# Attention weights of two head groups in six blocks: exponentials from query-by-key scores, turned in 32 by 32 squares and gathered through DRAM

## Chip, core and metric

The kernel runs on one core of one Trainium2 chip. The time is the device time of one execution in microseconds; the median of the runs shown stands for the kernel. The core has a matmul engine (PE, with PEld its weight loads), VectorE (DVE), ScalarE (ACT), GpSimd (POOL) and SyncE (SP), which issues nearly all DMAs of this kernel; 16 DMA engines move the data.

## What is computed

One transformer block with adaptive layer norm, in float32, on 8 sequences of 1024 tokens and 512 features; 16 heads of 32 features each, causal attention, a hidden layer of 2048 with gelu.

```python
mod = silu(cond) @ Wada + bada                     # 8 x 3072, split in six
sh_a, sc_a, gt_a, sh_m, sc_m, gt_m = split(mod, 6)
xm = layernorm(x, g1, be1) * (1 + sc_a) + sh_a
q, k, v = split_heads(xm @ Wqkv)                   # 16 heads of 32
scores = where(causal, q @ k.T / sqrt(32), -inf)
x = x + gt_a * (merge_heads(softmax(scores) @ v) @ Wproj + bproj)
xm = layernorm(x, g2, be2) * (1 + sc_m) + sh_m
x = x + gt_m * (gelu(xm @ W1 + b1) @ W2 + b2)
```

## The kernel before

**Tiling.** The 8 sequences are cut into 16 blocks of 512 tokens; block n is half h = n % 2 of sequence n // 2. A block of half 0 attends to its own 512 keys alone, in a causal triangle; a block of half 1 also to the 512 keys before. The 16 heads form four groups g of four heads (4 × 32 = 128 partitions). Queries, keys (`qTs`, `kTs`) lie features on partitions, values (`vs`) tokens on partitions. The large matrices (projections, hidden layer) run as Strassen products on halves, in the helper of L217, with weights streamed through a ring of 8 tiles of 256 KB (`wp`, fetched on SP at L358 to L362).

**An order written at build time.** All loops run in Python while the program is built. The instructions of each engine are laid down in one order that is fixed then, by a planner: `now` holds a modelled time of each engine and of the DMA queue, `written` and `left` when a datum is ready or free, `note`, `note_pe`, `note_act`, `note_dma` (L90 to L135) advance them with durations written in by hand. A DMA is modelled as beginning 1.0 us after its issue, landing 1.2 us after its transfer. Work that may wait is a generator (`start`, `sides`); it yields what it needs next. `work` (L1423) advances the thread with the shortest modelled wait. `step_aside` (L1457) and `until` lay linear work (matrices) in front of a piece of attention that isn't ready, and `pace` spreads a block's attention over the linear work planned for it (`planned_time`). On the chip each engine then runs its own instructions strictly in this order, and a semaphore that isn't there yet stops the engine.

**Attention before.** For each group the scores are computed twice. First by query (`scores_at_once`, L1595): 128 queries on partitions, keys along the row, in a PSUM buffer `st` of 4 heads × 512 columns; VectorE adds the triangle mask (L1607) and takes the row maxima (L1610). The maxima are split into three bf16 parts (`split_maxima`, on POOL or DVE) and turned by small matmuls (`maxima_rows`, L1648), so that they lie along the queries. Then by key (`weights_T`): keys on partitions, queries along the row; the matmuls of L1674 put the negative maxima into `st`, those of L1686 add the scores, ScalarE takes one exponential over 128 x 2048 (L1698) into an SBUF buffer `pT` (three slots, `free_p`), POOL cuts the triangle (L1703). This orientation is what the product with the values needs (`weigh`, L1726, into PSUM `po`). POOL adds the weights of all key tiles (`add_weights`, L1816); in `finish` a matmul with ones sums them over the keys (L1747), ScalarE copies sum and values to SBUF (L1756, L1759), VectorE inverts in four pieces (L1765), POOL multiplies (L1790) into `qTs`, from where the output projection reads.

**Units.** In a triangle the widths are 512, 384, 256 and 128 columns per head. They are packed into `st` as units: 512; 384 + 128; and one that two neighbouring groups share, 256 + 256. So a pair of groups in a block of half 0 has five units by query and five by key.

**DRAM detours that are there already.** `turn` (L700 to L714) turns normalized rows in 32 by 32 squares on VectorE, writes them to DRAM in one DMA of 1 MB (`held`) and reads them back in four of 256 KB.

Of the kernel before, what the change touches and what calls it, by code (L numbers as in the profile page):

```python
# [9 lines left out]
F32 = mybir.dt.float32  # L10
# [12 lines left out]
def kernel(  # L23
# [413 lines left out]

    cond_act = tmp.tile([P, TB], F32, tag="top", name="cond_act", bufs=1)[:B, :]
    nc.scalar.activation(cond_act, cond_sb, AF.Silu)
# [113 lines left out]
    def add_job(job, reads, first=False):  # L553

        at = sum(1 for other in jobs if other[2]) if first else len(jobs)
        jobs.insert(at, (job, reads, first))

    def run_jobs(everything=False):
# [37 lines left out]
    def hurry():  # L596

        while jobs and due(jobs[0][1]) <= now["PE"] + 500:
# [881 lines left out]
    TRIANGLE = [[0], [1, 3], [2]]  # L1480
    groups = [(n, g) for n in range(NB) for g in range(NC)]

# [175 lines left out]

    free_p = list(range(3))
    first_end, unadded = (0, NC - 1), []  # L1660
    outs, totals = {}, {}

    def weights_T(n, g, parts):
# [18 lines left out]
        for k, c0, w, gg in parts:  # L1682
# [53 lines left out]
    def finish(n, g):  # L1736
# [7 lines left out]
        for i, (c0, w, term, held) in enumerate(terms):  # L1744
# [6 lines left out]
            note_pe(2 * COLUMN * w, "columns", [("acc", n, g), ("p", held)], [("l", bank)])  # L1751
        free_p.extend([slot, *(held for *_, held in more)])
        top = tmp.tile([P, TB], F32, tag="top", name=f"top_{n}_{g}", bufs=1)
        rec = tmp.tile([P, TB], F32, tag="rec", name=f"rec_{n}_{g}", bufs=1)
        kr = "rec"
# [20 lines left out]
        if (n, g) == first_end:  # L1776
# [5 lines left out]
            return  # L1782

        def quotient():
            invert(3)
# [33 lines left out]
    def attend():  # L1819
        previous = None  # L1820
        for n in range(NB):
            h = blocks[n][1]
            slots = []
            mine = sum(exp_need(parts) for g in range(NC) for parts in weight_units(n, g))
            for g in range(NC):
                nxt = groups.index((n, g)) + 1
                n_slots = len(weight_units(n, g))

                over = n_slots - 1 if g % 2 == 0 else n_slots
                for k in range(n_slots):  # L1830
                    upto = len(units)
                    if nxt < len(groups):
# [4 lines left out]
                        if k == n_slots - 1 and nxt + 1 < len(groups):  # L1837
# [3 lines left out]
            stream["rate"] = planned_time(n) / mine * (0.7 if n == 0 else 1.0)  # L1841
            written["free for k", n + 2 if n % 2 else n + 1] = 0.0
# [31 lines left out]
    def close(n, g, parts, pT, slot, last):  # L1874

        until(lambda: n - blocks[n][1] + parts[-1][0] // NTT in valued)
        own, other = [[part for part in parts if (part[3] == g) == of] for of in (True, False)]
        weigh(n, g, own, pT, slot, last)
        if other:
            shared[n, g + 1] = other, pT, slot  # L1880
        elif parts[0][0] > 0 and (n, g) != first_end:
            free_p.append(slot)
        if parts[0][0] == 0:
            totals[n, g] = (pT, slot)
            if (n, g) in shared:
                more, pT, slot = shared.pop((n, g))
                weigh(n, g, more, pT, slot, False)
                add_weights(n, g, more, pT, slot)
                if (n, g) != first_end:
                    free_p.append(slot)  # L1890
        if last:
            finish(n, g)

    def next_scores():
# [15 lines left out]

    needs = sum(exp_need(parts) for n in range(NB) for g in range(NC) for parts in weight_units(n, g))
    needs += sum(score_need(*unit) for unit in units)
    for n in range(NB):
# [80 lines left out]
```

## Time and profile before

| | |
|---|---|
| runs of the kernel | 3505.2, 3508.09, 3507.78 us; median 3507.78 |
| profiled execution | 3510.74 us, its span 3509.0, granted PE clock 0.998 |
| instructions | 120365 |
| DMA | 491.10 MB, mean 140 GB/s |
| share of the 16 DMA engines, SP's queue | 47.1% |

The profile's page gives busy time by engine, then groups of instructions by source line; the chain of waits follows the work that ended last back from release to release; a view by stretches gives busy time of each engine in a window, with clock, DMA share and GB/s; a timeline lists instructions in order, start and duration in us. A float32 matmul appears as two instructions, and four heads run side by side in 32-row or 32-column parts of the array, so one piece of a unit is 8 matmul instructions (4 in bf16). The duration of a matmul contains the depth of the pipeline; what it costs in a stream is read from start to start.

### The profile page before, as it was taken

What the parts mean: (1) busy time and instruction counts of PE and PEld (TensorE: products, weight loads), DVE (VectorE), ACT (ScalarE), POOL (GpSimd) and SP (SyncE); (2) the same over time, 40 slices, a digit from 0 to 9 for tenths busy, and PEclk for the clock granted to TensorE, in tenths of its full rate; (3) what the DMA queues carried; (4) which work ended last, traced back from release to release, by engine and by line L of the source; (5) the groups of instructions that cost most, each with busy time, mean ns of one, the idle gap of its engine ahead of it and who ended that gap; (6) DMA issues with size and microseconds to landing.
All of it is one profiled execution on the core that took longest, in us unless ns stands there. A gap on an engine that the chain in (4) does not pass through costs nothing.

```text
span 3509.0 us, 120365 instructions
## 1 busy us (share of the span) xinstructions
PE 3454.3 (98%) x54429; PEld 1724.0 (49%) x54429; DVE 2198.9 (63%) x2401; ACT 1212.4 (35%) x1276; POOL 2084.2 (59%) x2258
## 2 busy tenths in 40 slices
PE   8999999999999999999999999999999999999999
PEld 4444445445554545445454454544555444554445
DVE  5766676564666656665666566765666756656563
ACT  2335333342233423335223342333423343232531
POOL 3767846666366663756727576275753658537660
PEclk9999999999999999999999999999999999999999
DMA  6843444535545445363454534545354544443334
GB/s 212 263 137 104 137 115 140 142 107 159 142 125 156 119 147 153 119 170 115 137 157 130 155 117 144 150 137 148 116 155 137 165 122 146 128 136 101 96 121 140
DMA packets 328194, 491.10 MB, mean 140 GB/s; under 512 B 27260, under 2 KB 177596, under 8 KB 324100
## 3 DMA queue, kind: packets, MB, share of 16 engines
q1 hardware_dynamic: 327568, 483.39, 47.1%
q8 instruction: 428, 7.01, 0.8%
q14 instruction: 82, 0.67, 0.1%
q10 hardware_dynamic: 116, 0.03, 0.0%
HBM read 425.57 MB, written 55.64 MB: 137 GB/s over the span
## 4 chain that ended last, share of the span: by engine, by line
PE 83%; POOL 7%; DMA 3%; DVE 3%; ACT 1%; issue 1%; SPq 1%; ACTq 0%; DVEq 0%; POOLq 0%
PE bank L217 59%; PE sc L1595 8%; PE st L1686 6%; PE po L1726 6%; POOL pT L1816 4%; PE st L1674 2%; PE bank L1747 2%; DMA hat_m<-held_m 1%; DVE mx L1610 1%; POOL hT L170 1%; ACT pT L1698 1%; DMA held_m<-xm_m 1%; PE bank L1648 0%; POOL xr L170 0%; DMA w<-in_L_cond_Wqkv_dram 0%
## 5 line engine op out<-in xcount | busy, mean ns | idle before, releaser
L1816 POOL TENSOR_TENSOR pT<-pT,pT 128x256 f32<-128x256 f32 (+3 forms) x1254 | 1219.7, 1007 | 298.5 <-PE po L1726 181.6
L1698 ACT ACTIVATE pT<-st 128x2048 f32<-128x2048 f32 x288 | 540.9, 1878 | 1065.1 <-PE st L1686 959.8
L217 PE MATMUL bank<-w,hT 128*32 128x256 f32 x14336 | 823.7, 380 | 0.4 <-issue 0.4
L1610 DVE TENSOR_REDUCE mx<-sc 128x4 f32<-128x2048 f32 (+3 forms) x384 | 665.9, 1755 | 235.6 <-PE sc L1595 229.5
L217 PEld LDWEIGHTS bank<-w,hT 128*32 128x32 f32 x14336 | 446.7, 110 | 390.3 <-issue 105.8
L217 PE MATMUL bank<-xm_m,w 128*32 128x256 f32 x8192 | 498.6, 381 | 3.6 <-ACT xm_m L774 2.2
L217 PE MATMUL bank<-t_m,w 128*32 128x256 f32 x6144 | 382.4, 380 | 0.9 <-DVE t_m L786 0.6
L217 PEld LDWEIGHTS bank<-xm_m,w 128*32 128x32 f32 x8192 | 255.6, 110 | 231.2 <-issue 62.2
L1703 POOL TENSOR_SCALAR_AFFINE_SELECT pT<-pT 128x512 f32<-128x512 f32 x256 | 167.5, 672 | 331.9 <-ACT pT L1698 329.4
L1607 DVE TENSOR_TENSOR sc<-sc,mask 128x1024 f32<-128x1024 f32 (+1 forms) x160 | 162.8, 1018 | 293.3 <-PE sc L1595 237.8
L1595 PE MATMUL sc<-kT,qT 32*128 32x512 f32 (+3 forms) x3072 | 329.5, 521 | 4.3 <-ACT pT L1698 3.3
L1726 PE MATMUL po<-pT,v 128*32 128x512 f32 (+3 forms) x3048 | 301.6, 490 | 3.9 <-POOL pT L1703 3.9
L1686 PE MATMUL st<-qT,kT 32*128 32x512 f32 (+3 forms) x3072 | 300.8, 487 | 0.0
L217 PEld LDWEIGHTS bank<-t_m,w 128*32 128x32 f32 x6144 | 189.6, 110 | 172.9 <-issue 48.5
L1765 DVE RECIPROCAL rec<-rec 128x128 f32<-128x128 f32 x256 | 227.3, 922 | 48.2 <-ACT rec L1756 48.2
L217 PE MATMUL bank<-xm_a,w 128*32 128x256 f32 x3968 | 243.4, 382 | 0.4 <-DMA w<-in_L_cond_Wqkv_dram 0.4
L217 PE MATMUL bank<-w,qT 128*32 128x512 f32 x2048 | 237.0, 595 | 1.1 <-DMA w<-in_L_cond_Wproj_dram 0.7
L1595 PEld LDWEIGHTS sc<-kT,qT 32*128 32x128 f32 x3072 | 129.6, 183 | 188.2 <-issue 88.4
L208 DVE TENSOR_TENSOR hT<-bank,u_u 128x512 f32<-128x512 f32 x187 | 126.6, 686 | 105.8 <-PE bank L217 103.1
L217 PE MATMUL bank<-t_a,w 128*32 128x256 f32 x2944 | 183.2, 380 | 0.0
L217 PEld LDWEIGHTS bank<-xm_a,w 128*32 128x32 f32 x3968 | 123.5, 110 | 110.3 <-issue 29.3
L1115 ACT ACTIVATE hT<-hT,cols 128x512 f32<-128x512 f32 x256 | 164.7, 712 | 35.9 <-DVE hT L208 28.5
(243 smaller groups left out, 3404.0 us busy)
## 6 DMA issues: line engine op xcount, KB each, us to landing
w<-in_L_cond_W_dram SPq DMA_DIRECT2D x384, 256.0 KB
w<-kept_up_S SPq DMA_DIRECT2D x256, 256.0 KB
w<-kept_down_S SPq DMA_DIRECT2D x256, 256.0 KB
w<-kept_qkv_S SPq DMA_DIRECT2D x180, 256.0 KB
w<-in_L_cond_Wqkv_dram SPq DMA_DIRECT2D x147, 256.0 KB
hat_a<-in_x_dram SPq DMA_DIRECT2D x64, 256.0 KB
xr<-in_x_dram SPq DMA_DIRECT2D x32, 512.0 KB
w<-in_L_cond_Wproj_dram SPq DMA_DIRECT2D x64, 256.0 KB
```

What stands on the lines that cost most here:

```text
L208: nc.vector.tensor_tensor(out, src, other, op)
L217: nc.tensor.matmul(ps[r, :], columns, rhs, start=start, stop=stop, skip_group_check=True)
L1115: nc.scalar.activation(hT[:, i, :], hT[:, i, :], AF.Gelu, bias=cols[:, O_B1 + f : O_B1 + f + 1])
L1595: nc.tensor.matmul(sc[:, j, c0 : c0 + w], qTs[n][r, gg, ts(qt, P)], keys_of(n, kh)[r, gg, :w], start=True, stop=True, skip_group_check=True,)
L1607: nc.vector.tensor_tensor(place, place, shape_of.to_broadcast(place.shape), ALU.add)
L1610: nc.vector.tensor_reduce(maxima[n, gg][:, kh, qt, :], sc[:, :, c0 : c0 + w], axis=AX.X, op=ALU.max)
L1686: nc.tensor.matmul(st[:, j, c0 : c0 + w], kT[r, gg, ts(k % NTT, P)], qT[r, gg, TB - w :], start=False, stop=True, skip_group_check=True,)
L1698: nc.scalar.activation(pT[:, :, :used], st[:, :, :used], AF.Exp, scale=scale)
L1703: nc.gpsimd.affine_select(diagonal, diagonal, pattern=[[0, HPG], [1, P]], compare_op=ALU.is_ge, fill=0.0, base=0, channel_multiplier=-1,)
L1726: nc.tensor.matmul(po[r, TB - w :], v[:, k % NTT, g * P + j * hd : g * P + (j + 1) * hd], pT[:, j, c0 : c0 + w], start=(k == 0), stop=last ...
L1765: nc.vector.reciprocal(some, some)
L1816: nc.gpsimd.tensor_tensor(into, into, pT[:, j, c0 : c0 + w], ALU.add)
```

## The change

For groups 0 and 1 of the blocks n = 4, 6, 8, 10, 12, 14 (`row_groups`), the weights are taken from the scores by query, and the scores by key are not computed. Of each row unit (`rows_unit`): scores by query, mask and maxima as before; then ScalarE takes one exponential per head and part, with the negative maximum as bias and the row sum as a second output, written so that 32 by 32 squares are in place; VectorE turns all squares of 128 x 2048 (`turned`); SP writes them in four DMAs of 256 KB to a DRAM image and reads the image back in one DMA of 1 MB into a slot of `pp` (`spread_unit`), whose layout has keys on partitions; the values are multiplied in pieces of 128 columns. The row sums are inverted and spread along the queries through DRAM, five small DMAs per group (`inverses`), and one product per group with the inverse ends it (`finish_rows`). So for these groups the subtracted maxima, second scores, triangle cuts, additions on POOL, sums by ones and long reciprocals are gone.

The row units run at the start of their block (`attend_rows`) over a share of 0.45 of its planned time; groups 2 and 3 follow as before, and their first values wait in the plan for the row groups' end (`close`). The three slots are shared. For all blocks the rule by which VectorE's waiting jobs are laid down (`run_jobs`) is looser: up to 2 us ahead of PE's modelled time. `top` and `rec` become halves of one buffer.

```diff
     def run_jobs(everything=False):
+        run_row_jobs(everything)
         while jobs and (
-            everything or (now["DVE"] <= now["PE"] and due(jobs[0][1]) <= now["PE"])
+            everything or (now["DVE"] <= now["PE"] + 2000 and due(jobs[0][1]) <= max(now["PE"], now["DVE"]))
         ):
...
-    groups = [(n, g) for n in range(NB) for g in range(NC)]
+    def row_groups(n):
+        return (0, 1) if n > 3 and blocks[n][1] == 0 else ()
...
+    groups = [(n, g) for n in range(NB) for g in range(NC) if g not in row_groups(n)]
...
-        slot = free_p.pop(0)
+        until(lambda: free_p)
+        slot = take_slot()
...
         until(lambda: n - blocks[n][1] + parts[-1][0] // NTT in valued)
+        if by_rows(n):
+            until(lambda: (n, row_groups(n)[-1]) in gathered)
...
+    SHARE = 0.45
...
+    def rows_unit(n, g, parts):
+        until(lambda: n in projected)
+        until(lambda: free_p and len(raws) < 2)
...
+        for i, (qt, kh, c0, w, gg) in enumerate(parts):
+            nc.vector.tensor_reduce(mx[:, i, :], sc[:, :, c0 : c0 + w], axis=AX.X, op=ALU.max)
+            note("DVE", 170 + 4.14 * w, ["st"], [("mxr", slot)])
+        nc.vector.tensor_scalar(minus[:, :n_parts], mx[:, :n_parts], -scale, None, ALU.mult)
...
+            for j in range(HPG):
+                nc.scalar.activation(
+                    tile_of[:, j], sc[:, j, c0 : c0 + w].rearrange("p (k b x) -> p k b x", b=NTT, x=hd),
+                    AF.Exp, bias=minus[:, i, j : j + 1], scale=scale, accum_out=totals_of[n, gg][:, j, qt : qt + 1],
+                )
+                note_act(480 + 0.82 * w, "exp", ["st", ("mxr", slot)], [("p", slot)])
...
+        def turned():
+            nc.vector.transpose(raw, raw)
+            note("DVE", 2320, [("p", slot)], [("p", slot)])
+            written["p", slot] += 1500
+            start(spread_unit(n, raw, slot, parts, order_of[n, g, parts[0][0]]))
+        row_jobs.append((turned, [("p", slot)]))
+
+    def spread_unit(n, raw, slot, parts, i):
+        yield [("p", slot)], []
+        image = kept.tile([P, NTT, TB], F32, tag=f"image_{i % 5}", name=f"image_{n}_{i}")
+        for a in range(NTT):
+            into = image[:, a, :].rearrange("(b x) r -> x b r", x=hd)
+            nc.sync.dma_start(into, raw[ts(a, hd)].rearrange("x (b r) -> x b r", b=NTT))
+            note_dma(700, [("p", slot)], [("image", n, i)])
+        left["p", slot] = now["DMA"] + LAND
+        written["image", n, i] += 1500
...
+        page = pp.tile([P, NTT, TB], F32, tag=f"p{taken_slot}", name=f"turned_{n}_{i}")
+        nc.sync.dma_start(page, image)
+        note_dma(2700, [("image", n, i)], [key])
+        written[key] += 2000
+        if i:
+            yield [("valued rows", n, i - 1)], []
+        for qt, kh, c0, w, gg in parts:
...
+            for k in range(w // P):
...
+                for j in range(HPG):
+                    r = slice(j * hd, (j + 1) * hd)
+                    at = c0 + k * P + j * hd
+                    nc.tensor.matmul(
+                        out[0][r, ts(qt, P)],
+                        vs[n][:, k, gg * P + j * hd : gg * P + (j + 1) * hd],
+                        page[:, :, at : at + hd],
+                        start=out[1] == 1,
+                        stop=out[1] == 10,
+                        skip_group_check=True,
+                    )
+                note_pe(2 * COLUMN * P, "columns", [key], ["po"])
+            if out[1] == 10:
+                finish_rows(n, gg, out[0])
...
+    def inverses(n, g):
...
+        nc.vector.reciprocal(some, some)
...
+        nc.vector.transpose(both[:, 1, :].rearrange("p (y i) -> p y i", i=hd), wide)
...
+            nc.sync.dma_start(both[ts(j, hd), 0, :], row.to_broadcast([hd, TB]))
...
+    def finish_rows(n, g, out):
+        into = qTs[n][:, g, :]
+        if wait_of(([("inverses", n, g)], [])) > 0 or max(now["DVE"], due(["po"])) > max(now["ACT"], due(["po"])) + 2500:
+            nc.scalar.copy(into, out)
+            note_act(585, None, ["po"], [("values", n, g)])
+            start(scaled(n, g, into))
+        else:
+            nc.vector.tensor_tensor(into, out, inverse_rows.pop((n, g)), ALU.mult)
```

More of the change, by code (lines that the diff above doesn't have):

```diff
@@ new lines, in row_need, with attend_rows @@
+    def row_need(n, g, parts):
+        return score_need(n, g, parts) + 400 + 1900 * sum(part[3] for part in parts) / TB
+    def attend_rows(n, previous):
+        todo = row_units(n)
+        lo = unit_at[0]
+        more = MORE
+        ends = [lo + i * 0 // (len(todo) - 1) for i in range(len(todo))]
+        mine = sum(row_need(n, *unit) for unit in todo)
+        mine += sum(score_need(*unit) for unit in units[lo : ends[-1]])
+        stream["rate"] = SHARE * planned_time(n) / mine
+        written["free for k", n + 1] = 0.0
+        for g in row_groups(n):
+            written["spread", n, g] = NEVER
+            written["sums", n, g] = NEVER
+            written["inverses", n, g] = NEVER
+            in_sums[n, g] = 0
+        for (g, parts), upto in zip(todo, ends):
+            rows_unit(n, g, parts)
+            run_excursions(1)
+            pace(row_need(n, g, parts))
+            if previous is not None:
+                close(*previous)
+                previous = None
+                for i in (n, n + 1):
+                    written["free for v", i] = 0.0
+            while unit_at[0] < upto:
+                ns = score_need(*units[unit_at[0]])
+                next_scores()
+                run_excursions(1)
+                pace(ns)
+            maxima_rows()
@@ new lines, in inverses @@
+    def inverses(n, g):
+        before = [("spread", n, g - 1)] if g else []
+        yield [("sums", n, g), "top used", *before], ["top", "rec"]
+        both = tmp.tile([P, 2, TB], F32, tag="top", name=f"inverse_{n}_{g}", bufs=1)
+        some = totals_of.pop((n, g))
+        nc.vector.reciprocal(some, some)
+        note("DVE", 170, [("sums", n, g)], [("sums", n, g)])
+        wide = some.rearrange("p j t -> p (j t)").unsqueeze(2).to_broadcast([P, HPG * NTT, hd])
+        nc.vector.transpose(both[:, 1, :].rearrange("p (y i) -> p y i", i=hd), wide)
+        note("DVE", 700, [("sums", n, g)], ["rec"])
+        yield ["rec"], []
+        rows = kept.tile([HPG, NTT, NTT, hd], F32, tag=f"inverse_{g % 2}", name=f"inverse_rows_{n}_{g}")
+        nc.sync.dma_start(
+            rows.rearrange("j t a i -> a (j t) i"),
+            both[0:P:hd, 1, :].rearrange("a (y i) -> a y i", i=hd),
+        )
+        note_dma(150, ["rec"], [("rows back", n, g)])
+        yield [("rows back", n, g)], []
+        for j in range(HPG):
+            row = rows[j : j + 1].rearrange("j t a i -> j (t a i)")
+            nc.sync.dma_start(both[ts(j, hd), 0, :], row.to_broadcast([hd, TB]))
+            note_dma(200, [], ["top"])
+        inverse_rows[n, g] = both[:, 0, :]
+        written["inverses", n, g] = written["top"] + LATE / 2
```

139 lines of the change are left out of this document (126 added, 13 removed).

## The prediction

> **What bounds the kernel now.** I read the page first, then the busy time by stretches, then the TensorE timeline of some units.
>
> ```profile
> span 3509.0 us, 120365 instructions
> ...
> PE 3454.3 (98%) x54429; PEld 1724.0 (49%) x54429; DVE 2198.9 (63%) x2401; ACT 1212.4 (35%) x1276; POOL 2084.2 (59%) x2258
> ...
> DMA packets 328194, 491.10 MB, mean 140 GB/s; under 512 B 27260, under 2 KB 177596, under 8 KB 324100
> ...
> PE 83%; POOL 7%; DMA 3%; DVE 3%; ACT 1%; issue 1%; SPq 1%; ACTq 0%; DVEq 0%; POOLq 0%
> ```
>
> The matmul engine is busy 98% of the span and makes 83% of the chain that ended last; no other engine reaches 65%. The stretches say whether that holds where the change acts. Below are the stretch from 500 to 3350 us, then the sum row of six stretches in which groups 0 and 1 of blocks 4, 6, 8, 10, 12 and 14 run today (from the end of the block before to the end of group 1: 770 to 870, 1200 to 1295, and so on, 561 us together).
>
> ```profile
> 500.00:3350.00 2850.00, 2832.54 (x44551) 1411.91 (x44544) 1780.19 (x1915) 1007.55 (x1056) 1714.17 (x1846) 1.00 0.47 137
> ...
> 1200.00:1295.00 95.00, 94.53 (x1546) 48.79 (x1536) 56.91 (x56) 26.43 (x25) 75.44 (x73) 1.00 0.49 151
> ...
> sum 561.00, PE 556.56 PEld 278.91 DVE 338.17 ACT 160.24 POOL 438.95; mean PE 92.76 PEld 46.48 DVE 56.36 ACT 26.71 POOL 73.16
> ```
>
> PE idles 17.5 of 2850 us in the middle and 4.4 of 561 us in the six stretches, at clock 1.00. So a microsecond of matmul taken out there is a microsecond of time, as long as PE finds its next work ready. Busy ends are modelled, so I price by start-to-start, not by busy.
>
> **What is removed from PE.** Per pair of groups five key-by-query score units with the subtracted maxima (L1674, L1686), two sums by ones (L1747), two turns of the maxima (L1648). From the PE timeline, a unit of each shape and the next start:
>
> ```profile
> 976.07 0.40 PE L1674 MATMUL st<-mrow,minus_ones 32*128 32x384 bf16 x8
> ...
> 977.32 0.64 PE L217 MATMUL bank<-t_m,w 128*32 128x256 f32 x8
> ...
> 980.36 0.41 PE L1648 MATMUL bank<-ident_b,mcols 128*32 128x128 bf16 x16
> 980.59 1.47 PE L1726 MATMUL po<-pT,v 128*32 128x512 f32 x16
> ```
>
> ```profile
> 1051.81 0.40 PE L1674 MATMUL st<-mrow,minus_ones 32*128 32x256 bf16 x8
> ...
> 1053.00 1.92 PE L217 MATMUL bank<-w,qT 128*32 128x512 f32 x16
> ...
> 1059.51 0.40 PE L1674 MATMUL st<-mrow,minus_ones 32*128 32x512 bf16 x4
> ...
> 1060.69 1.50 PE L217 MATMUL bank<-w,qT 128*32 128x512 f32 x12
> ```
>
> The 384+128 unit takes 977.32 − 976.07 = 1.25 us, the shared 256+256 unit 1053.00 − 1051.81 = 1.19, the 512 unit 1060.69 − 1059.51 = 1.18; a pair has two, one and two: 2 × 1.25 + 1.19 + 2 × 1.18 = 6.05. A turn of maxima takes 980.59 − 980.36 = 0.23. The ones-sum has its price in the chain of waits:
>
> ```profile
> 1054.93 0.86 PE po L1726 x16
> ...
> 1066.91 0.86 PE bank L1747 x8
> ```
>
> 0.86 each. Per pair: 6.05 + 2 × 0.23 + 2 × 0.86 = 8.23 us; six pairs: **49.4 us**.
>
> **What is added to PE.** The scores by query (L1595) are computed as before, once, so they cost nothing new. The values (L1726) keep their columns: ten pieces of 128 per head and group in place of 512+384+256+128, both 1280. A pair's five units, 512 columns a head each, cost 5 × 0.86 = 4.3 today. Twenty pieces of 128 at a quarter of 0.86 (0.215) are 4.3 again; that a 128 behind a 384 already costs no more is the x16 line (0.86 for 384+128). The upper bound is the busy time of the single 128 form:
>
> ```profile
> L1726 PE MATMUL po<-pT,v 128*32 128x128 f32 x504 | 25.3, 273 | 0.2 <-POOL pT L1703 0.2
> ```
>
> 25.3 us over 63 sets of eight is 0.40 each, so 20 × 0.40 = 8.0: at worst +3.7 a pair, +22 in all. I take 0: the turns of L1648 put four sets of 128 columns, sixteen weight loads, into 0.23 us, so loads at this rate are not the limit there (they are bf16, which is why the upper end stays in the range). Reading the page in runs of 32 elements shows in no row; it belongs to the same bounds.
>
> The Trainium skill (TensorE: Matmul & The Clock Gate, Back-to-back issue gap) gives for streams of weight load and matmul about 81 ns at 128 columns against 56 ns alone. By that ratio, as an estimate, the pieces would cost 1.45 times as much, 6.2 us a pair, and the sum would be 12 us worse; the trace's 128 columns behind 384 do not show it, and a row of 128s after another is not in this trace.
>
> **What is added elsewhere, and hidden.**
>
> ```profile
> L1816 POOL TENSOR_TENSOR pT<-pT,pT 128x256 f32<-128x256 f32 (+3 forms) x1254 | 1219.7, 1007 | 298.5 <-PE po L1726 181.6 <-ACT pT L1698 114.5
> L1698 ACT ACTIVATE pT<-st 128x2048 f32<-128x2048 f32 x288 | 540.9, 1878 | 1065.1 <-PE st L1686 959.8 <-POOL pT L1816 54.1 <-POOL mcols L1631 23.7
> ...
> L1765 DVE RECIPROCAL rec<-rec 128x128 f32<-128x128 f32 x256 | 227.3, 922 | 48.2 <-ACT rec L1756 48.2
> ...
> L1115 ACT ACTIVATE hT<-hT,cols 128x512 f32<-128x512 f32 x256 | 164.7, 712 | 35.9 <-DVE hT L208 28.5 <-POOL hT L170 6.7
> ...
> L700 DVE STREAM_TRANSPOSE xm_a<-hat_a 128x512 f32<-128x512 f32 x56 | 35.1, 674 | 0.0
> ```
>
> ScalarE: five exponentials of 1.88 become 32 small ones a pair with a bias per row. L1115 has such a bias: 0.712 at 512 wide; 2048 wide at 1.878 bounds the slope at 0.78 to 0.92 ns an element, so 384, 256 and 128 come to about 0.60, 0.49, 0.38, and the 32 to 8 × 0.71 + 8 × (0.60 + 0.38) + 8 × 0.49 = 17.4 us. The read-out of the sums has no row: 0 to 0.2 us each, 0 to 6. Less 9.4 for the old ones: +8 to +14 a pair, in a stretch where ACT is busy 160 of 561 us. Hidden.
>
> VectorE: five turns of 2048 at 4 × 0.674 = 2.7 (13.5), against eight reciprocals of 0.92 (7.4); with the small inverse and two products about +9 a pair, on 338 of 561 busy. Hidden by matmuls in other banks; without that cover it would be the 54 us of six pairs. POOL loses 24 additions at about 1.0, eight triangle cuts and two products, some 30 us a pair: worth nothing directly, since PE hardly waits for it.
>
> The score buffer (one, tag "st") is now held through the exponentials, 2.9 us for the 512 unit and 3.9 for the others; in exchange the second unit's 1.2 on PE and 1.9 on ACT no longer take it: about level.
>
> DMA: each of 30 units writes 1 MB of squares in four transfers and reads 1 MB back, plus five small ones per group: 210 more issues on SP, at 0.42 as below 88 us of a queue that otherwise waits for free ring pieces. The nearest rows are today's turns of x through DRAM (one write of 1 MB, four reads of 256 KB); SP's issues, the chain, and what PE lost:
>
> ```profile
> 1255.43 0.42 SPq L709 DMA_DIRECT2D held_a<-xm_a  x1
> ```
>
> ```profile
> 1255.43 5.38 DMA held_a<-xm_a
> ...
> 1263.06 6.04 DMA hat_a<-held_a
> 1269.25 2.23 ACT xm_a L774 x3
> ```
>
> ```profile
> 1274.26 3.66 PE L217 MATMUL bank<-w,xm_a 128*32 128x256 f32 x64 [0.47 <-ACT p_v L197]
> ```
>
> That trip took 13.8 us (1255.43 to 1269.25) against 12.0 in the planner's figures (1.0 + 2.6 + 1.2 and 1.0 + 4 × 1.25 + 1.2), and PE lost 0.47. The new trip runs the other way: the first leg is four writes from 32 partitions each, like today's reads, the second one transfer of 1 MB, like today's write. Planned are 1.0 + 4 × 0.7 + 1.2 + 1.5 and 1.0 + 2.7 + 1.2 + 2.0 = 13.4 us with their margins, so at today's 13.8 it would overrun by 0.4, not by 1.8. Two waits are new. On SP the read of a page waits for its image to land; behind it stand weight loads, for which PE waits, but the ring holds eight pieces of 32 instructions each, 1.8 us a piece by the last row (64 in 3.66), 14 us in all. On PE the first value matmul of a unit waits for its page, and everything in order on PE stands behind it. I take 0.5 us of lost PE a unit, next to the 0.47, since the smaller overrun meets a busier queue: 15 us. Bounds: 0, and 0.8 (all 17.5 us of middle idle over the 22 or so trips there), 24 us.
>
> The planner's looser rule for VectorE's jobs touches all 16 blocks; I take 0, between a gain of the few microseconds idle and a loss of the same.
>
> **Sum.** −49.4 + 0 + 15 = −34.4 us, against the profiled execution's 3510.7 (its span plus 1.7): 3476.3. That execution is 3.0 above the median of the runs, so 3507.8 − 34.4 = **3473**.
>
> **Rivals.** *Late pages (slower).* PE's order is fixed beforehand, so a page later than planned is lost PE time, 30 times. 491 MB take 47% of 3509 us today, 3.4 us a MB; 10.5 MB a pair in about 93 us add 0.38 to a share of 0.48: 0.86. If that stretches a trip by a fifth (13.8 to 16.4 us) and PE pays the whole overrun, it loses 3 us a unit, 90 in all: 3507.8 − 49.4 + 90 = 3548. It decides from 49.4 / 30 = 1.65 us a unit. For it: the plan leaves no room at share 0.49. Against, too, that an overrun of 1.8 cost PE only 0.47 above. And the busiest 50 us for DMA behind the first 200 leave PE no idle time:
>
> ```profile
> 800.00:850.00 50.00, 49.97 (x884) 28.22 (x884) 29.88 (x31) 9.40 (x11) 34.95 (x33) 1.00 0.69 210
> ```
>
> *Attention falls behind (no change).* Values of groups 2 and 3 now wait in the plan for the last row unit, some 27 us (9 in the score buffer, 2.7 turn, 14 trip). If the matrices cover three quarters, 6.75 us a block go idle, 40.5 in all: −49.4 + 15 + 40.5 = +6: 3514. Against: PE is covered by matrices in all six stretches today.
>
> *Dear pieces.* Values at 0.40 a piece: −49.4 + 22 + 15 = −12: 3495.
>
> That the change does nothing is excluded: the choice of blocks is fixed in the code.
>
> **How the numbers follow.** The forecast has 0.60, dear pieces 0.12, attention behind 0.10, late pages 0.18. The range: 3455 (no stall, and a few us of other waits gone) to 3516, which takes in the middle rivals and leaves out the late pages; the forecast's own range is 3456 to 3486. Beyond 0.2% (7 us), about what a measurement can tell, lie the forecast and dear pieces below, 0.72; attention behind stays within, 0.10; late pages above, 0.18.
>
> **What would show it.** L1674, L1686, L1747 and L1648 fall by 12 of 64 groups' share; the values get a 128x128 form at about 0.215 us a set; PE stays at 98% busy. Wrong if PE idles before the value matmuls with a DMA as releaser, if weight loads release PE in the six stretches, or if DMA share there passes 0.9.

## The result, and the profile after

| | median us | runs | ratio to before, 95% interval |
|---|---|---|---|
| before | 3507.39 | 3505.2 to 3508.09 | |
| after | 3535.7 | 3534.38 to 3539.84 | 1.008 [1.0069, 1.0092] |

The change costs 28 us where 34 were forecast as a gain. The page of the changed kernel:

```profile
span 3538.1 us, 120328 instructions
...
PE 3420.3 (97%) x54141; PEld 1720.4 (49%) x54141; DVE 2281.0 (64%) x2522; ACT 1202.6 (34%) x1537; POOL 1964.6 (56%) x2016
...
DMA packets 352916, 557.28 MB, mean 158 GB/s; under 512 B 31244, under 2 KB 181580, under 8 KB 344980
...
PE 78%; DMA 8%; DVE 6%; POOL 3%; issue 2%; ACT 1%; SPq 1%; ACTq 0%; DVEq 0%; POOLq 0%
```

PE's busy time fell by 34.0 us, but its idle time (span less busy) rose from 54.7 to 117.8. DMA went from 3% to 8% of the chain of waits. The view by stretches, with the six windows in which the row units of the changed kernel run (three of them and the sum; columns: window, length, busy time of PE, PEld, DVE, ACT, POOL with instruction counts, clock, DMA share, GB/s):

```profile
820.00:930.00 110.00, 102.52 (x1720) 54.48 (x1720) 77.88 (x93) 31.79 (x82) 45.78 (x40) 0.97 0.83 254
...
2135.00:2230.00 95.00, 86.24 (x1461) 46.47 (x1462) 62.94 (x81) 28.07 (x73) 36.31 (x39) 0.98 0.89 270
...
3005.00:3095.00 90.00, 77.45 (x1294) 40.79 (x1287) 54.13 (x71) 23.56 (x55) 29.83 (x35) 0.98 0.87 268
sum 590.00, PE 532.42 PEld 283.85 DVE 385.13 ACT 164.41 POOL 216.96; mean PE 88.74 PEld 47.31 DVE 64.19 ACT 27.40 POOL 36.16
```

PE is idle 590.00 − 532.42 = 57.6 us there, at a DMA share of 0.83 to 0.89 and below full clock. What it waits for, by the view of waits (PE alone: total us, times, longest):

```profile
PE bank L217 <- DMA w<-in_L_cond_Wproj_dram: 27.3, 13, 3.5
PE po L2096 <- DMA turned<-image: 14.5, 10, 3.4
PE bank L217 <- DVE p_v L194: 10.5, 6, 1.9
```

The weights of the output projection cost nearly twice what the pages (`turned`) do. (The third line stands at 10.5 with a quarter of the trips' bytes too, and at 3.2 in the last run below, so it goes with the planner's rule.) The weights' row on the page of the kernel before ended in 1.1 us of idle time:

```profile
L217 PE MATMUL bank<-w,qT 128*32 128x512 f32 x2048 | 237.0, 595 | 1.1 <-DMA w<-in_L_cond_Wproj_dram 0.7
```

One such wait in the changed kernel, in the chain of waits (start, duration, what):

```profile
2152.00 11.50 DMA out_dram<-xr
2163.57 5.69 DMA w<-in_L_cond_Wproj_dram
```

in the timeline of SP's issues:

```profile
2152.00 0.48 SPq L1180 DMA_DIRECT2D out_dram<-xr  x1
2155.27 2.98 SPq L362 DMA_DIRECT2D w<-in_L_cond_Wproj_dram  x2
2158.94 3.09 SPq L2064 DMA_DIRECT2D image<-rows_p  x4
2162.28 1.14 SPq L1180 DMA_DIRECT2D out_dram<-xr  x1
2163.57 2.29 SPq L362 DMA_DIRECT2D w<-in_L_cond_Wproj_dram  x2
```

and in the timeline of PE:

```profile
2164.30 3.18 PE L217 MATMUL bank<-w,qT 128*32 128x512 f32 x16 [3.13 <-DMA w<-in_L_cond_Wproj_dram]
...
2169.31 1.06 PE L217 MATMUL bank<-w,qT 128*32 128x512 f32 x8 [1.82 <-DMA w<-in_L_cond_Wproj_dram]
...
2203.26 1.08 PE L2096 MATMUL po<-turned,v 128*32 128x128 f32 x32
2204.16 0.61 PE L217 MATMUL bank<-xm_a,w 128*32 128x256 f32 x8
...
2218.93 1.08 PE L2096 MATMUL po<-turned,v 128*32 128x128 f32 x32 [1.19 <-DMA turned<-image]
```

The chain goes from a store of 512 KB that took 11.50 us to a weight piece issued at 2163.57, only after it; that piece, 256 KB, took 5.69 us more, and the matmul of 2169.31 had waited 1.82 for it. The piece does not read what the store wrote. But in the trace SP's DMAs use eight semaphores in turn, and SP waits for a semaphore's last DMA before it issues the next one with it: an issue waits until the eighth one before it has landed. The store of 2152.00 is the eighth before the piece of 2163.57, and of the seven between them four are writes of a row trip. (This order comes with the program; it is no measured limit of the chip's queue.) So slow landings make later issues late, and the ring of about 14 us of weights does not cover them. SP's own waits show weight loads held by page reads that they do not use (line, total us, times, longest); in the kernel before no single DMA holds these two lines for more than 1.9 us in total:

```profile
SPq L360 <- DMA turned<-image: 11.0, 4, 4.1
SPq L362 <- DMA turned<-image: 10.0, 4, 3.4
```

The landings are slow where the engines are full, which the mean share of 0.83 to 0.89 hides; by windows of 5 us (window, length, PE busy, clock, DMA share, which this view can put above 1 in a short window, GB/s):

```profile
2155.00:2160.00 5.00, 4.21 (x80) 1.00 1.07 196
2160.00:2165.00 5.00, 1.87 (x32) 0.98 1.06 395
2165.00:2170.00 5.00, 3.18 (x20) 0.68 0.96 329
```

In windows of 2 us the share is 0.95 or more in 56% of these six stretches, in 14% of the prediction's six stretches of the kernel before, and in 26% of the stretches with a quarter of the bytes (below).

**A second loss, before any row trip.** The view of the down-projection's matmuls (`bank<-w,hT`, 896 a block) gives a mark, the same piece of work in every kernel: the first one of block 2. (What is laid ahead of it differs little: 11617 matmul instructions in the changed kernel, 11585 before.) In the kernel before (duration min/median/max, first and last start):

```profile
L217 PE MATMUL bank<-w,hT x896: 379/379/403, 772.8 to 839.9; 128*32 128x256 f32 x180
```

and after:

```profile
L217 PE MATMUL bank<-w,hT x896: 379/379/403, 786.0 to 849.8; 128*32 128x256 f32 x180
```

The changed kernel is already 13.2 us behind, though its first row unit begins at 820.0. Three runs below with the same rule and as many matmul instructions up to the mark stand at 780.2 to 782.2, so 7.4 to 13.2 is what single profiles show. What remains, from the mark to the end, was 2736.2 us and is 3538.1 − 786.0 = 2752.1, 15.9 more. One of the early stalls, in PE's timeline of the changed kernel:

```profile
436.26 1.14 PE L1617 MATMUL sc<-kT,qT 32*128 32x512 f32 x8 [0.99 <-ACT pT L1736]
440.60 0.39 PE L1711 MATMUL st<-mrow,minus_ones 32*128 32x512 bf16 x4 [3.21 <-DVE mx L1632]
```

and VectorE's order at that place:

```profile
433.56 0.85 DVE L167 TENSOR_TENSOR xr<-xr,row_gba 128x512 f32<-128x512 f32 x1
437.52 0.70 DVE L1629 TENSOR_TENSOR sc<-sc,mask 128x512 f32<-128x512 f32 x1 [3.11 <-issue]
438.25 2.29 DVE L1632 TENSOR_REDUCE mx<-sc 128x4 f32<-128x2048 f32 x1
```

VectorE is through with its waiting jobs early and stands idle 3.11 us; PE issues the scores at 436.26, and its next instruction, which uses their maxima, waits 3.21 us for mask and maxima, with no matmul of other work laid in between. (Which of the moved jobs made the plan so was not followed.) The gap has an echo, in the view by stretches of 2 us (window, length, PE busy, clock, DMA share, GB/s):

```profile
440.00:442.00 2.00, 1.40 (x12) 0.78 0.00 0
442.00:444.00 2.00, 2.00 (x16) 0.50 0.00 0
444.00:446.00 2.00, 2.00 (x20) 0.87 0.00 0
446.00:448.00 2.00, 2.00 (x24) 1.00 0.03 8
```

After the gap PE runs at half clock for about 3.4 us: 2 × (0.22 + 0.50 + 0.13) = 1.7 us are lost beyond the 3.21, and they stand as busy time, not as idle time. The Trainium skill (TensorE: Matmul & The Clock Gate, Part 1: The HAM clock gate) gives half clock after an idle window of about 3.4 us, and full clock again after about as long a busy one. The length of the slow stretch agrees, but here an idle time of 3.21 us by the profile was enough, and one of 2.50 us ahead of 1294.26 too (clock 0.61 from 1294 to 1296).

### The profile page after: what moved, and what is told of

The parts are those of the page before. It is cut to its first block, busy times and chain, and to the rows that moved or that the text cites. A ratio compares the mean times of both kernels' runs of the same rounds, so it can differ in the third digit from the quotient of the medians.

```text
span 3538.1 us, 120328 instructions
## 1 busy us (share of the span) xinstructions
PE 3420.3 (97%) x54141; PEld 1720.4 (49%) x54141; DVE 2281.0 (64%) x2522; ACT 1202.6 (34%) x1537; POOL 1964.6 (56%) x2016
## 4 chain that ended last, share of the span: by engine, by line
PE 78%; DMA 8%; DVE 6%; POOL 3%; issue 2%; ACT 1%; SPq 1%; ACTq 0%; DVEq 0%; POOLq 0%
PE bank L217 54%; PE sc L1617 7%; PE po L1764 6%; PE st L1723 5%; DMA turned<-image 3%; PE st L1711 2%; POOL pT L1858 2%; DVE mx L1632 1%; PE bank L1785 1%; DMA w<-in_L_cond_Wproj_dram 1%; DMA out_dram<-xr 1%; DMA hat_m<-held_m 1%; PE rows_sc L2021 1%; DMA held_m<-xm_m 1%; PE po L2096 1%
## 5 line engine op out<-in xcount | busy, mean ns | idle before, releaser
L1858 POOL TENSOR_TENSOR pT<-pT,pT 128x512 f32<-128x512 f32 (+3 forms) x1110 | 1127.5, 1052 | 257.1 <-ACT pT L1736 138.2
L1736 ACT ACTIVATE pT<-st 128x2048 f32<-128x2048 f32 x258 | 484.7, 1879 | 873.3 <-PE st L1723 795.3
L1632 DVE TENSOR_REDUCE mx<-sc 128x4 f32<-128x2048 f32 (+3 forms) x335 | 592.6, 1788 | 179.2 <-PE sc L1617 174.6
L1741 POOL TENSOR_SCALAR_AFFINE_SELECT pT<-pT 128x512 f32<-128x512 f32 x208 | 141.3, 697 | 356.7 <-ACT pT L1736 328.4
L1617 PE MATMUL sc<-kT,qT 32*128 32x512 f32 (+3 forms) x2680 | 296.4, 530 | 10.9 <-DVE mx L1632 5.3
L1629 DVE TENSOR_TENSOR sc<-sc,mask 128x1024 f32<-128x1024 f32 (+1 forms) x129 | 131.4, 1019 | 259.8 <-PE sc L1617 194.6
L1764 PE MATMUL po<-pT,v 128*32 128x512 f32 (+3 forms) x2664 | 270.5, 497 | 0.4 <-issue 0.4
L1723 PE MATMUL st<-qT,kT 32*128 32x512 f32 (+3 forms) x2688 | 270.3, 494 | 0.0
L217 PE MATMUL bank<-w,qT 128*32 128x512 f32 x2048 | 242.2, 608 | 27.3 <-DMA w<-in_L_cond_Wproj_dram 27.3
L2040 ACT ACTIVATE rows_p<-rows_sc,rows_minus 128x512 f32<-128x512 f32 (+3 forms) x192 | 98.4, 535 | 332.9 <-DVE rows_minus L2034 260.9
L1804 DVE RECIPROCAL top_rec<-top_rec 128x128 f32<-128x128 f32 x208 | 187.3, 926 | 31.3 <-ACT top_rec L1795 31.3
```

The costliest lines, as they stand in the source:

```text
L217: nc.tensor.matmul(ps[r, :], columns, rhs, start=start, stop=stop, skip_group_check=True)
L1617: nc.tensor.matmul(sc[:, j, c0 : c0 + w], qTs[n][r, gg, ts(qt, P)], keys_of(n, kh)[r, gg, :w], start=True, stop=True, skip_group_check=True,)
L1629: nc.vector.tensor_tensor(place, place, shape_of.to_broadcast(place.shape), ALU.add)
L1632: nc.vector.tensor_reduce(maxima[n, gg][:, kh, qt, :], sc[:, :, c0 : c0 + w], axis=AX.X, op=ALU.max)
L1723: nc.tensor.matmul(st[:, j, c0 : c0 + w], kT[r, gg, ts(k % NTT, P)], qT[r, gg, TB - w :], start=False, stop=True, skip_group_check=True,)
L1736: nc.scalar.activation(pT[:, :, :used], st[:, :, :used], AF.Exp, scale=scale)
```

## The experiments

Three theories stood against each other. *A*: the trips' bytes fill the DMA engines in six stretches, so that weights and pages land late. *B*: SP's queue, in order, holds weight loads behind waiting page reads. *C*: the planner's new rules cost time by themselves (*C1*: the looser rule for VectorE's jobs; *C2*: its other edits).

**The planner alone.** The changed kernel with no row groups at all:

```diff
-        return (0, 1) if n > 3 and blocks[n][1] == 0 else ()
+        return ()
```

> The changed kernel with no row groups at all: every group takes the old way, but the looser rule for VectorE's jobs, the shared slots and the halves of one buffer stay. Theory A (transfers: the row trips fill the 16 DMA engines in six stretches, so pages and weights land late) and theory B (queue: SP issues in order and stops at a read whose image has not landed, with weight loads behind it) both expect the time of the kernel before, 3507 us within 7. Theory C (planner: the new rules lay work down worse in all 16 blocks) expects most of the loss to stay: above 3525.

Measured 3534.93 us, 1.0079 [1.0064, 1.0094]: the time of the full change, without the change's purpose. That is C; A and B expected 3507. (The theories do not exclude each other: this run shows what the rules cost without row groups, and not that the trips cost nothing.)

**A quarter of the bytes.** Each trip keeps its issues, their order and its place, but writes and reads only a quarter of each row. The output leaves out the other three quarters of the squares' way.

```diff
-        image = kept.tile([P, NTT, TB], F32, ...)
+        image = kept.tile([P, NTT, P], F32, ...)
...
-            nc.sync.dma_start(into, raw[ts(a, hd)].rearrange("x (b r) -> x b r", b=NTT))
+            nc.sync.dma_start(into, raw[ts(a, hd)].rearrange("x (b r) -> x b r", b=NTT)[:, :, :P])
...
+        page = page[:, 0, :].rearrange("p (a r) -> p a r", a=NTT)
         nc.sync.dma_start(page, image)
...
-                    at = c0 + k * P + j * hd
+                    at = j * hd
```

> The changed kernel with the same instructions in the same order on every engine, but each row trip moves a quarter: 4 x 64 KB out and 256 KB back, and the value matmuls read that quarter for all their pieces (the remaining weights are left out of the sum). Theory A: the DMA share in the six stretches falls from about 0.86 to about 0.6, the 57 us of PE idle there mostly vanish and the clock stays at 1.00, so 3535 - 57 - 15 = 3463, at most 3480. Theory B: the waits on SP stay, only shorter, so at most half is won back: above 3500. Theory C: 3530 or more.

Measured 3475.71 us, 0.9913 [0.9897, 0.993]. Its DMA total is 510.10 MB, 47.2 less than after, and 60.0 us went with them. In its own six stretches, view by stretches:

```profile
2520.00:2620.00 100.00, 97.67 (x1680) 53.30 (x1675) 69.64 (x87) 28.98 (x75) 38.80 (x43) 1.00 0.68 194
...
sum 610.00, PE 595.10 PEld 321.93 DVE 428.40 ACT 177.05 POOL 259.80; mean PE 99.18 PEld 53.65 DVE 71.40 ACT 29.51 POOL 43.30
```

PE idles 14.9 of 610 us at shares of 0.63 to 0.68, clock 1.00. The page waits are gone, and the row of the projection's weights shows 2.3 of idle time. Since issues and order are the same, it is the bytes: A, and B only as far as SP waits for transfers that the bytes made long. The spans differ by 65.8 us (3538.1 to 3472.3): 48.7 of them are less idle time of PE, of which the projection's weights make 25.0 and the pages 14.5, and 17.1 are less busy time for the same 54141 matmul instructions (3420.3 to 3403.2). The latter is the clock: its mean over the span is 0.992 in the changed kernel and 0.997 here, by which some 18 us are to be expected (an estimate: 0.008 × 3538 less 0.003 × 3472).

**Another queue, and no image.** First the trips' DMAs issued by POOL in place of SP:

```diff
-            nc.sync.dma_start(into, raw[ts(a, hd)]...)
+            nc.gpsimd.dma_start(into, raw[ts(a, hd)]...)
...
-        nc.sync.dma_start(page, image)
+        nc.gpsimd.dma_start(page, image)
```

(and the five small ones of the inverses likewise).

> The changed kernel with the row trips' transfers and the inverses' (11 per unit pair side, 210 in all) issued by POOL in place of SP; same bytes, same order on PE. Theory A: the DMA engines are as full as before, so 3525 to 3545. Theory B: weight loads are no longer behind a waiting read, the 26 us of late projection weights and part of the late pages vanish: 3500 or less. If POOL's own waits at these issues matter, its additions come late and the time rises above 3545.

Measured 3596.2 us, 1.0253 [1.0236, 1.0269], against the expectations of A and B alike; the third one, above 3545, came. In the view of waits POOL stands 10.5 us for images and 21.6 for inverses at its issues. PE's waits in this kernel:

```profile
PE po L2096 <- DMA turned<-image: 59.4, 17, 9.3
PE bank L217 <- DMA w<-in_L_cond_Wproj_dram: 28.7, 8, 7.0
```

With no page read in front of them on SP, the projection's weights were as late as before (28.7 against 27.3), and the pages later. One such piece in the chain of waits:

```profile
1288.81 10.84 DMA w<-in_L_cond_Wproj_dram
```

The six late pieces in the row stretches took 10.8 to 14.6 us from issue to landing here, the eleven of the changed kernel 5.2 to 9.2, after SP had held several of them back. So B falls as the sole reason of the late weights: a waiting SP is one way in which full engines make them late, and without it each transfer takes longer. (This run changes the queue of the trips as well as SP's order, so the two parts are not split cleanly.) The Trainium skill (DMA: Bandwidth & Descriptors, Issuing engines are not separate DMA queues) says that all issuing engines share the 16 DMA engines and that another queue saves issue time alone. The 28.7 us agree. The kernel as a whole lost another 60 us by the move.

Then squares moved straight from SBUF to SBUF, sixteen DMAs of 64 KB a unit, no DRAM image:

```diff
-        image = kept.tile([P, NTT, TB], F32, ...)
...
-        nc.sync.dma_start(page, image)
...
+        for a in range(NTT):
+            for b in range(NTT):
+                nc.sync.dma_start(page[ts(b, hd), a, :], raw[ts(a, hd), ts(b, TB)])
```

> The changed kernel without the DRAM image: the turned squares go from SBUF to SBUF straight into the page, in 16 transfers of 64 KB per unit (480 issues on SP in place of 150), half the bytes and one landing in place of two; the planner lays it down anew with 16 x 0.17 us per unit. Theory A: the load added in the six stretches halves (share about 0.7), so half or more of the 72 us lost there comes back: 3470 to 3500. Theory B: three times the issues in front of the weight loads: 3530 or more.

Measured 3658.89 us, 1.0431 [1.0415, 1.0446]: half the bytes of the trips (525.88 MB in all) and the worst time, B's side of the expectation and not A's. 480 issues took SP 0.59 us each (median), 9.4 us a unit. The view of waits:

```profile
PE po L2092 <- DMA turned<-rows_p: 66.5, 17, 5.7
PE sc L1617 <- ACT pT L1736: 30.7, 7, 6.7
```

So bytes are not the only price; many small issues on SP cost too. Which part is issue, which the small transfers themselves, and which that sixteen of them pass through SP's eight semaphores, was not separated.

**The rule for VectorE's jobs.** Added alone to the kernel before:

```diff
-            everything or (now["DVE"] <= now["PE"] and due(jobs[0][1]) <= now["PE"])
+            everything or (now["DVE"] <= now["PE"] + 2000 and due(jobs[0][1]) <= max(now["PE"], now["DVE"]))
```

> The kernel before with one line of the change: the looser rule for VectorE's jobs, all else untouched. Theory C1 (the looser rule alone makes the 27 us that e1 lost): 3535, at least 3525. Theory C2 (e1's loss comes from the other planner edits: halves of one buffer, slots): 3508 within 7.

Measured 3534.45 us, 1.0072 [1.0057, 1.0087]: C1, and C2 about nothing. Its mark (start of block 2's down-projection) stands at 782.2, 9.4 late; by the spans (3533.9 against 3509.0) the other 15.5 us come later.

The reverse, the changed kernel with the old rule:

> The changed kernel with the old rule for VectorE's jobs, row groups and their trips as in the change. C1: the 27 us come back, 3535 - 27 = 3508 (3500 to 3516), and the six stretches keep their idle PE and late weights. C2: 3535 within 10.

Measured 3568.68 us, 1.0174 [1.0159, 1.019], against expectation: 33 us worse than after. Its waits:

```profile
PE po L2096 <- DMA turned<-image: 57.0, 12, 8.7
```

In a kernel with row units the old rule leaves the pages later still (57.0 against 14.5). The same line is a loss of 27 in one kernel and a gain of 33 in the other.

**Spreading the rows.** SHARE, the part of the block's planned time given to row units, from 0.45 to 0.75; once with the looser rule, once with the old one:

```diff
-    SHARE = 0.45
+    SHARE = 0.75
```

> The changed kernel with the row units spread over 0.75 of the block's planned time in place of 0.45, looser rule kept. Theory A: the trips' 10.5 MB a block fall over some 160 us, DMA share there near 0.70 as in the quarter-byte run, so most of that run's 60 us comes back: 3480 to 3505. If the loss hangs on where a trip meets the projection weights and not on the mean share, less than half comes back: above 3510.

> Both: the old rule and the row units over 0.75 of the block. If A and C1 hold and add, 3535 - 27 - 30 to 50 = 3458 to 3478, faster than both kernels. If either falls, 3500 or more.

Measured 3513.05 us, 1.0014 [1.0003, 1.0024], and 3546.41 us, 1.0113 [1.0096, 1.013]. Spreading wins about 22 us under either rule: the same bytes over a longer stretch. That is less than half of the 60 us, where A expected most of them, and the second run stays above 3500, so A and C1 do not simply add. In the first of the two, the view by stretches has for block 4:

```profile
820.00:980.00 160.00, 151.62 (x2604) 83.52 (x2600) 98.74 (x123) 47.78 (x101) 49.62 (x49) 0.99 0.73 224
```

The share is 0.73 over 160 us, where it was 0.83 over 110. A lower mean is not enough: the projection's weights still cost 11.1 us of waiting and the pages 8.7.

**The looser rule only while rows are in work**, the old one elsewhere:

```diff
-            everything or (now["DVE"] <= now["PE"] + 2000 and due(jobs[0][1]) <= max(now["PE"], now["DVE"]))
+            everything or (now["DVE"] <= now["PE"] + 2000 * rowing[0] and due(jobs[0][1]) <= max(now["PE"], now["DVE"] * rowing[0]))
```

with `rowing[0]` set to 1 at the start of `attend_rows` and to 0 when the last row group is gathered.

> The changed kernel, but VectorE's looser job rule holds only while a block's units of groups 0 and 1 are in work (from the first row unit until group 1 is gathered); everywhere else the old rule. Sum of the runs so far: the looser rule costs +26 us where no rows are in work (e5_before_rule against the kernel before) and is worth 33 us where they are (e6_old_rule against the changed kernel). If the two places are separate: 3535 - 26 = 3509 us, give or take 6. If the looser rule's loss lies in the blocks with rows as well: about 3525. If it needs the looser rule outside the stretches too (work run ahead of them): 3550 or more.

> As e9_stretch_rule, and the row units spread over three quarters of the block's planned time (SHARE 0.75 instead of 0.45). e7_share won 22 us over the changed kernel by the same step. If the two gains add: 3535 - 26 - 22 = 3487 us, which beats the kernel before by 20. If spreading makes the stretches so long that the looser rule is in force nearly everywhere, the 26 us come back: about 3510.

Measured 3529.08 us, 1.0063 [1.004, 1.0087], and with SHARE 0.75 3511.46 us, 1.0008 [0.9999, 1.0018]. The main expectations (3509 and 3487) were 20 us and more too good; the alternatives that they named, 3525 and 3510, lie near. The mark of the first shows what was gained, in the view of the down-projection:

```profile
L217 PE MATMUL bank<-w,hT x896: 378/379/404, 771.0 to 837.7; 128*32 128x256 f32 x180
```

The early loss is gone (771.0 against 772.8 before), and by the profiles that is all there was to gain: from the mark to the end it takes 3525.0 − 771.0 = 2754.0, as after (2752.1). By the medians only 6.6 us are gained, since the profiled run of the changed kernel was its slowest. Behind the mark, then, the looser rule outside the row stretches costs the changed kernel nothing that shows. Whether the later part of the 26 us is absent from this kernel or lies in the stretches in which the rule stays, these runs do not tell; a sum over two kernels was the wrong sum either way.

**Both costs out.** First the old rule with quarter bytes:

> The changed kernel with the old rule for VectorE's jobs everywhere and a quarter of the bytes in each row trip (the output leaves out the other three quarters of the squares' way). If bytes and rule are independent: e2_bytes 3476 + (3569 - 3535) = 3509. If the looser rule is worth its 33 us only because it covers for late transfers, it is a loss again once the bytes are gone: 3476 - 26 = 3450, which is also what the sum of the prediction would be with free trips (3507 - 49 = 3458).

Measured 3494.91 us, 0.9957 [0.9943, 0.9972], between the two expectations: with light trips the looser rule is still worth 19 us (3495 to 3476), and in the waits pages are late by 19.7 us under the old rule though the bytes are few. So the rule helps the row units themselves and not only against full DMA engines. Then quarter bytes and the looser rule only while rows are in work:

> The changed kernel with both suspected costs out: a quarter of the bytes in each row trip (the output leaves out the other three quarters of the squares' way), and the looser rule for VectorE's jobs only while units of groups 0 and 1 are in work. By intervals between every 896th down-projection matmul, e2_bytes stands 9 us behind the kernel before in the first 550 us, where no row trip has yet been made, and 47 us ahead of it in the rest. If these two are the whole story, the first 9 go and the 47 stay: 3508 - 47 = 3461 us, give or take 6, which is the forecast's 49.4 us with next to nothing lost to the trips. If the looser rule outside the stretches is what lets the quarter trips be hidden (as e9_stretch_rule's 3529 instead of 3509 could mean): 3476 or more, no better than e2_bytes.

Measured 3460.53 us, 0.9866 [0.985, 0.9882]; 3461 were expected. That it fits to the microsecond is luck in part: from the median of the quarter bytes alone, 3475.7 less the 9 us at the mark make 3467. (The expectation's "first 550 us" are the time up to the mark: 781.9 with quarter bytes alone, 772.8 before.) Its mark, then two rows of its page, the engines and the projection's weights:

```profile
L217 PE MATMUL bank<-w,hT x896: 379/379/403, 770.7 to 837.3; 128*32 128x256 f32 x180
```

```profile
PE 3396.8 (98%) x54141; PEld 1708.9 (49%) x54141; DVE 2260.9 (65%) x2493; ACT 1222.8 (35%) x1562; POOL 1952.1 (56%) x2012
...
L217 PE MATMUL bank<-w,qT 128*32 128x512 f32 x2048 | 236.2, 594 | 0.9 <-DMA w<-in_L_cond_Wproj_dram 0.9
```

From the mark to the end of its span (3457.8) are 2687.1 us, 49.1 less than the 2736.2 of the kernel before. PE has the same 54141 instructions as in the changed kernel and is busy 23.5 us less (3420.3 − 3396.8). The same matmuls took longer in the changed kernel, and half clock after gaps, as at 440, is nearly all of that: at mean clocks of 0.992 and 0.998 some 21 us are to be expected (an estimate: 0.008 × 3538 less 0.002 × 3458).

## Why the prediction was wrong, by its steps

**The 49.4 us of removed matmul work held.** With light trips and the rule kept away from the other work, 49.1 us come out from the mark to the end by the profiles, and 46.9 of the whole by the medians (46.0 against the runs of the kernel before that were made beside it). That it meets 49.4 so closely is luck in part: PE's busy time fell by 57.5 us (3454.3 to 3396.8) and its idle time rose by 6.3, and a quarter of the trips is still in it.

**The pieces of 128 columns at nothing held.** In the timeline above, 32 matmuls (four sets) start at 2203.26 and the next work at 2204.16: 0.225 us a set against the 0.215 taken; the 17 runs of 32 in this trace that the next work follows at once have a median of 0.224. The rival *Dear pieces* (0.40) falls, and the 0.31 that the 81-to-56 ratio of the Trainium skill (TensorE: Matmul & The Clock Gate, Back-to-back issue gap) would give is not seen either.

**The failed step: "I take 0.5 us of lost PE a unit … 15 us".** Against light trips the full bytes cost 60 us (3535.7 to 3475.7), 2.0 a unit, past the 1.65 from which *Late pages* was to decide. The step looked at the page's trip alone, and took its delay from a trip on engines that were half idle. But the waits put 14.5 us on pages and 27.3 on projection weights, which the step held covered by a ring of 14 us: that holds for a piece that is issued in time and lands as usual, not where SP issues only once the eighth DMA before has landed and landing takes 5 to 9 us more. And gaps of this kind brought half clock behind them, about 17 of the 65.8 us between the spans, for which the step had no term. It worked out the share of 0.86, right by the 0.83 to 0.89 measured, and used it for the rival alone; today's detours, from which the 0.5 came, run at 0.49. *Late pages* had the right side and the right cause, the load on the DMA engines; but its 3548 priced the pages at 90 us and left out the weights, the clock and the rule, so that it lies 12 us from the measured time is luck. Of the three signs named, two came (a DMA as releaser ahead of the value matmuls, weight loads as releasers), the third (a share past 0.9) did not by the mean of a stretch, and did in the windows of 5 us around the waits (0.96 to 1.07).

**The second failed step: "The planner's looser rule … I take 0".** Away from the row units it costs the changed kernel about 15 us with light trips (3475.7 to 3460.5; 11.2 of it at the mark, 781.9 to 770.7, before any row trip) and 6.6 with full ones. Its bound, "the few microseconds idle", left out that the rule can make new idle time where there was none, and that a gap of about 3 us then costs half clock as well.

The books, by medians: 3507.4 − 46.9 (work removed, as in the last run) + 15.2 (rule) + 60.0 (bytes) = 3535.7. Each term is the difference of two runs on one path from before to after, so the sum must close and proves nothing by itself. The split between the last two depends on the order: with full bytes, taking the rule out of the other work wins 6.6 by the medians, and quarter bytes then 68.6.

**What held aside from that.** *Attention falls behind* is not what happened: with light trips the same order of groups 2 and 3 loses next to nothing. (Two of the prediction's figures are slightly off and decide nothing: the parts of its 27 us, 9 + 2.7 + 14, make 25.7, and the lower slope of the exponential is (1.878 − 0.712) / 1536, 0.76 ns and not 0.78.) VectorE's turn took 2.29 us where 2.7 were taken, and ScalarE, busy 164.41 of 590 us in the row stretches, is no bound:

```profile
L2051 DVE STREAM_TRANSPOSE rows_p<-rows_p 128x2048 f32<-128x2048 f32 x30 | 68.7, 2291 | 2.0 <-ACT rows_p L2040 1.4 <-DMA image<-rows_p 0.6
```

What stays open: no kernel here that computes everything beats the one before; the best two, with rows spread, stand within 0.2% of it. A smaller format for the squares, which would halve the bytes, an even larger share, and weight loads that don't share SP's eight semaphores with the trips were not tried. Why the looser rule helps the row units under light trips was not followed to the single wait.

## What to carry to other kernels

A DMA trip added beside a stream of prefetched weights is to be priced at the DMA share of its own stretch, in windows short enough to show full engines, and the price looked for at everything that shares the engines or the order of issue: here the weights paid more than the trip's own reader. Where a planner fixes the order, an edit of its rules is a change to every block; it is measured alone, and its worth in one kernel is not carried over to another. A mark at the same piece of work in all runs splits a loss by place before anything is theorized about it.

## What the runs showed of the hardware

- A gap of 3.21 us on PE was followed by about 3.4 us at half clock, and a gap of 2.50 us by half clock too. 3.4 us of it add 1.7 us to a stall, and show as busy time, not as idle time: PE's busy time is 17.1 us apart between full and quarter bytes.
- At a mean DMA share of 0.89 (0.96 to 1.07 in the windows around it) a store of 512 KB took 11.50 us in the chain of waits and a read of 256 KB 5.69.
- Issued by POOL in place of SP, the same trips left late weight pieces of 256 KB landing 10.8 to 14.6 us after their issue on SP, where it was 5.2 to 9.2.
- Squares of 64 KB sent from SBUF to SBUF cost more time than four times as large pieces by way of DRAM, at half the bytes (3658.89 against 3535.7 us).
- An exponential with a row sum is followed on ScalarE by a second instruction that reads the sum out, 0.21 us each:

```profile
L2040 ACT ACTIVATION_READ_ACCUMULATOR rows_p<-rows_sc,rows_minus 128x1 f32 x192 | 41.0, 213 | 0.0
```
